# A Mamba state laid out in halves: another partition order and another cut of the replicated loads

## The chip, the cores and the metric

The kernel runs on one core of a Trainium2 chip. The metric is the device time of one execution, in microseconds; lower is better. Its engines are named as in the profile: PE (matrix multiply), DVE (vector), ACT (scalar and activation), POOL (GpSimd), and SP, which here only issues DMAs.

## The reference, cut to what matters

Four layers follow each other on an input of 2 x 128 x 128 x 128 float32: a convolution with a small Mamba scan and a group norm, a gate from window statistics, the first layer's form again with other weights, and a residual block of two 3x3 convolutions. The change is in the Mamba scan, which runs in the first and the third layer. At each of the 2 x 128 x 128 positions the 128 channels are taken as 8 tokens of 16 features; a token has 32 inner features d and each of these 16 states n:

```python
seq = y.reshape(B * H * W, 8, 16)
...
dA = jnp.exp(dt[..., None] * A)                       # (N, 8, 32, 16)
dBx = dt[..., None] * Bm[:, :, None, :] * xc[..., None]
def step(h, inp):
    a, b, c = inp
    h = a * h + b
    return (h, jnp.sum(h * c[:, None, :], axis=-1))
_, ys = jax.lax.scan(step, h0, (dA, dBx, Cm))         # over the 8 tokens
ym = ys + D * xc
```

So B and C of a token depend on n alone, u = dt * xc on d alone, and the state on both.

## The kernel before, in words

A tile is 4 rows of the picture, 512 positions; there are 64 tiles in a scan and 128 in the two. The 32 x 16 = 512 states of a token stand as 4 planes (j) of 128 partitions. A partition holds one state n and one e of 8 (d is split into j and e); `_state(e)` says which 16 partitions belong to e. Constants and weights that are prepared ahead take their columns from it: `neg`, `red` and `alog`.

The state needs u spread over n and B, C spread over e. The kernel does it with DMAs through HBM: `store` (L382, L389) writes u into the scratch tensor `su` (8 DMAs of 64 KB) and B and C into `sb` (2 DMAs); `load` reads them back for each of the tokens 0 to 6, replicated, into `ur` (128 partitions x 4 x 512) and `bcr` (128 x 2 x 512). Before, 112 partitions hold 16 states times 7 values of e, and the last 16 hold the eighth e, so that each of the two tiles is loaded by a DMA of 112 and one of 16 partitions (L435, L436 for `ur`; L439, L440 for `bcr`).

For a token t the steps are:
- `inject` (L445, POOL): h = ur * B, one instruction over 128 x 2048;
- `decay` (L454 on PE, L463 on ACT): exp(dt * A) into PSUM, two tiles `set`;
- `token` (L472, L473, L477, DVE): for each half of the planes, the decayed state, its product with C into `r`, and the sum with the injected part into `h`. L477 of token t reads what `inject` of token t wrote; L472 of the first token reads what `inject` of token 0 wrote;
- `gather` (L492, PE): the sum over n.

The order of work on every engine is written out by hand: each step has a due time in units of a token (LOAD_AT, INJECT_AT and so on, 7 a tile), and the instructions are issued in that order. Loads are due 3.7 tokens before the tile's clock, injects 1.8 before; the store of a tile is due just ahead of its first load. All these DMAs are issued by SP, in order. `ur` has 3 buffers, `bcr` 5, `h` 4. A DMA waits for its buffer and its source, and also for the eighth DMA before it, since eight completion lanes are used in turn. After the conv, the projections and softplus (PE, ACT) of the next tile fill the gaps.

Of the kernel before, what the change touches and what calls it, by code (L numbers as in the profile page):

```python
# [31 lines left out]
P = 128  # L32
NT, FT = 8, 16
DI, DS, DC = 32, 16, 4
NQ = 4
NJ = DI * DS // P
DJ = DI // NJ
NG = 4
CG = P // NG
WIN = 8  # L40
ROWS = 4
NS = ROWS * P
# [7 lines left out]
def _constants(H):  # L50

    parts = {}

    neg = np.zeros((NJ, NQ, DJ, NQ, P), np.float32)
    red = np.zeros((P, NQ, NQ, DJ), np.float32)
    gsum = np.zeros((2, NQ, DS, 2, NJ, NQ, DJ), np.float32)
    for q in range(NQ):
        for e in range(DJ):
            neg[:, q, e, q, _state(e)] = -1.0
            red[_state(e), q, q, e] = 1.0  # L60
        for g in range(2):
            gsum[g, q, :, g, :, q, :] = 1.0
    parts["neg"] = neg.reshape(P, -1)
    parts["red"] = red.reshape(P, -1)
    parts["gsum"] = gsum.reshape(P, -1)
    parts["group"] = np.kron(np.eye(NG), np.full((CG, CG), 1.0 / CG)).astype(np.float32)
    parts["ident"] = np.eye(P, dtype=np.float32)
    parts["neghalf"] = np.full((P, CG), -0.5, np.float32)
    return _packed(parts)


def _state(e):


    return np.arange(DS) + P - DS if e == DJ - 1 else np.arange(DS) * (DJ - 1) + e


def _bilinear(n):
# [38 lines left out]
def _mamba_layout(w):  # L117
# [5 lines left out]
    def half(a):  # L123

        a = a.reshape(*a.shape[:-2], 2, NQ, NJ, DJ)
        return np.ascontiguousarray(np.swapaxes(a, -3, -2)).reshape(*a.shape[:-4], 2 * P)
# [18 lines left out]
    for q in range(NQ):  # L145
        pdt1[:, q, :, :, q, :] = by_d[0][:, :, None, None]
        pdt2[:, q, :, :, q, :] = w["dt_proj_w"][:, 0].reshape(NJ, DJ)[None, None, :, :]
        pb[:, q, :, q, :] = by_d[1 : 1 + DS].transpose(1, 2, 0)
        pc[:, q, :, q, :] = by_d[1 + DS :].transpose(1, 2, 0)
        for e in range(DJ):  # L150
            alog[:, q, e, q, _state(e)] = w["A_log"].reshape(NJ, DJ, DS)[:, e, :]
# [137 lines left out]
def _mamba(tc, src, w, con, dst, scratch, stats, H):  # L289


    nc = tc.nc
# [136 lines left out]
    def load(k, t):  # L429

        s = live[k]
        n = P - DS
        ur = s["ur", t] = st.tile([P, NJ, NS], F32, tag="ur", name="ur", bufs=3)
        u = s["su"][t]
        nc.sync.dma_start(out=ur[:n], in_=u[: DJ - 1].unsqueeze(0).to_broadcast([DS, DJ - 1, NJ, NS]))  # L435
        nc.sync.dma_start(out=ur[n:], in_=u[DJ - 1].unsqueeze(0).to_broadcast([DS, NJ, NS]))  # L436
        m = s["bc", t] = st.tile([P, 2, NS], F32, tag="bcr", name="bcr", bufs=5)
        b = s["sb"][t]
        nc.sync.dma_start(out=m[:n], in_=b.unsqueeze(1).to_broadcast([DS, DJ - 1, 2, NS]))  # L439
        nc.sync.dma_start(out=m[n:], in_=b)  # L440

    def inject(k, t):
        s = live[k]
# [103 lines left out]
    x1, z1 = ahead(1)[0], behind(1)[0]  # L547
    order = [(0, band)] + taps(0, 0, 9) + [(0, turn)] + x0 + taps(1, 0, 3) + dt0 + taps(1, 3, 5) + bc0
    order += [(0, load, 0), (0, load, 1), (0, load, 2)]
    order += z0 + taps(1, 5, 9) + [(1, turn), (0, decay, 1), (0, inject, 0), (0, inject, 1)] + own0  # L550
    order += x1[:2] + z1[:2]
# [7 lines left out]
    for k in range(len(src) * ntile):  # L559
# [20 lines left out]
        for t in range(NT - 1):  # L580
            put(k, LOAD_AT + t, load, t)
            put(k, INJECT_AT + t, inject, t)
# [37 lines left out]
def _gates(tc, src, w, con, y, stats, wm, b1, up, dst, H):  # L620
# [6 lines left out]
    with tc.tile_pool(name="dg", bufs=2) as dp, tc.tile_pool(name="dg1", bufs=1) as sp, tc.tile_pool(  # L627
# [58 lines left out]
        def gram(b, y0):  # L686
# [3 lines left out]
            pg = s["pg"] = psg.tile([P, 2, 512], F32, tag="pg", name="pg")  # L690
            tiles = [(a, a * P // 2, g * CG) for g in range(NG) for a in range(2)]
            for a, pa, c0 in tiles:
# [414 lines left out]
```

## Time and profile before

| What | Value |
|---|---|
| Median of 3 runs | 7580.34 us (7578.54 to 7589.2) |
| Span of the profiled execution | 7571.5 us |
| DVE busy | 7011.8 us, 93% |
| PE busy | 6319.0 us, 83% |
| POOL busy | 5499.8 us, 73% |
| ACT busy | 4282.3 us, 57% |
| DMA queue of SP | 568672 packets, 1747.28 MB, 88.1% of 16 engines |
| `ur` loads, issue to landing | 11.5 us (112 partitions, 896 KB), 11.1 us (16, 128 KB) |
| `bcr` loads, issue to landing | 11.7 us (112 partitions, 448 KB), 11.0 us (16, 64 KB) |

The span runs from the first to the last instruction of one profiled execution; the page gives that execution's time by its span alone, and the median of the runs is 8.8 us above it. Busy shares are averages over the whole span, the two scans and the stages between and after them. A group's row has its line, engine, operation, tiles and count, then busy time and mean ns of one, and last the time that the engine was idle just before such instructions, with what ended most of it. The share of a DMA queue is the time that its packets took, of sixteen engines' span.

### The profile page before, as it was taken

Reading aid. Unit: us, or ns where it says so; the run is one execution under the profiler, and the core shown is the slowest. Engines: PE = TensorE matmul, PEld = TensorE weight load, DVE = VectorE, ACT = ScalarE, POOL = GpSimd, SP = SyncE. Lnnn points to the kernel's source line nnn. Section 1 sums busy time; section 2 is a strip of 40 time slices with the busy share of each in tenths; the row PEclk is TensorE's granted clock in tenths of the full one; section 3 lists DMA queues with packets and bytes.
Section 4 is the critical chain, followed back from the end, with each engine's and each line's share of the span. In section 5 each row is a group of like instructions: output and inputs, shape, how many; then the busy total and the mean of one; then the engine's idle time right before and its main releaser. Section 6 shows DMA issues by size and latency. Waiting matters only on the chain.

```text
span 7571.5 us, 89536 instructions
## 1 busy us (share of the span) xinstructions
PE 6319.0 (83%) x30416; PEld 2335.1 (31%) x30416; DVE 7011.8 (93%) x7114; ACT 4282.3 (57%) x4877; POOL 5499.8 (73%) x1783
## 2 busy tenths in 40 slices
PE   7888888888888888867788888888888888887994
PEld 2222222222222222224222222222222222223873
DVE  5999999999999999978699999999999999999986
ACT  5666666666656656545556666666656655662222
POOL 5878777877787778754578777877787778775541
PEclk8999999999999999978899999999999999997997
DMA  8999999999999999954799999999999999996604
GB/s 204 252 251 252 251 250 246 256 251 253 246 248 254 250 243 249 245 194 173 193 249 247 250 250 249 250 256 246 249 252 252 251 245 253 249 253 199 207 7 172
DMA packets 573738, 1769.80 MB, mean 234 GB/s; under 512 B 85568, under 2 KB 239712, under 8 KB 458208
## 3 DMA queue, kind: packets, MB, share of 16 engines
q1 hardware_dynamic: 568672, 1747.28, 88.1%
q10 hardware_dynamic: 4608, 16.78, 0.6%
q8 instruction: 242, 3.96, 0.2%
q14 instruction: 216, 1.77, 0.1%
HBM read 1552.83 MB, written 210.89 MB: 233 GB/s over the span
## 4 chain that ended last, share of the span: by engine, by line
DVE 41%; DMA 25%; PE 19%; issue 7%; ACT 5%; POOL 2%; SPq 1%; POOLq 0%; DVEq 0%; ACTq 0%
DMA bcr<-sb 19%; DVE set L472 14%; DVE h L477 12%; DVE r L473 12%; PE m L911 6%; DMA ur<-su 3%; PE one L350 2%; PE set L454 2%; ACT set L463 2%; PE ys L492 2%; PE one L400 2%; POOL h L445 2%; DVE v L505 1%; PE ys L483 1%; ACT xc L357 1%
## 5 line engine op out<-in xcount | busy, mean ns | idle before, releaser
L445 POOL TENSOR_TENSOR h<-ur,bcr 128x2048 f32<-128x2048 f32 x896 | 4060.7, 4539 | 1257.0 <-DMA bcr<-sb 1096.1
L472 DVE TENSOR_TENSOR set<-set,h 128x1024 f32<-128x1024 f32 x1792 | 2193.5, 1224 | 267.6 <-ACT set L463 165.4
L473 DVE TENSOR_TENSOR r<-set,bcr 128x1024 f32<-128x1024 f32 x1792 | 2194.5, 1225 | 61.5
L463 ACT ACTIVATE set<-set 128x1024 f32<-128x1024 f32 x1792 | 1745.9, 1006 | 870.0 <-PE set L454 856.6
L477 DVE TENSOR_TENSOR h<-set,h 128x1024 f32<-128x1024 f32 x1536 | 1866.0, 1215 | 28.1 <-POOL h L445 27.8
L454 PE MATMUL set<-dt,rep 32*128 32x512 f32 x7168 | 1402.9, 675 | 104.9 <-DVE h L477 98.1
L492 PE MATMUL ys<-r,ct 128*32 128x512 f32 x7168 | 1172.5, 635 | 36.4 <-DVE r L473 36.1
L323 PE MATMUL one<-band,conv 128*128 128x512 f32 x2304 | 1081.3, 605 | 21.9 <-DMA band<-in_x_dram 12.6
L454 PEld LDWEIGHTS set<-dt,rep 32*128 32x128 f32 x7168 | 405.1, 193 | 1002.3 <-issue 468.1
L400 PE MATMUL one<-xc,keep 128*64 128x512 f32 x1008 | 322.4, 723 | 462.1 <-ACT xc L357 355.5
L323 PEld LDWEIGHTS one<-band,conv 128*128 128x128 f32 x2304 | 406.6, 189 | 668.0 <-issue 596.8
L911 PE MATMUL m<-comb,u 128*128 128x256 f32 x2304 | 507.8, 381 | 46.0 <-DVE comb L904 44.8
L483 PE MATMUL ys<-t,ct 128*128 128x512 f32 x512 | 322.6, 716 | 252.3 <-DVE v L505 250.7
L911 PEld LDWEIGHTS m<-comb,u 128*128 128x128 f32 x2304 | 436.2, 190 | 117.3 <-issue 54.5
L492 PEld LDWEIGHTS ys<-r,ct 128*32 128x32 f32 x7168 | 181.2, 112 | 929.2 <-issue 759.6
L352 ACT ACTIVATE xc<-one,keep 128x512 f32<-128x512 f32 x252 | 173.4, 688 | 509.2 <-PE one L350 504.2
L374 POOL TENSOR_TENSOR u<-dt,xc 128x1024 f32<-128x1024 f32 x128 | 302.8, 2365 | 98.0 <-ACT dt L368 98.0
L420 PE MATMUL one<-prod,ct 128*128 128x512 f32 x504 | 280.8, 640 | 109.1 <-POOL prod L412 78.8
L350 PE MATMUL one<-y,w_in 128*128 128x512 f32 x504 | 341.1, 765 | 1.6 <-ACT xc L352 1.6
L463 ACT ACT_TABLE_LOAD x254 | 325.9, 1283 | 4.5
L427 POOL TENSOR_TENSOR t<-t,xc 128x1024 f32<-128x1024 f32 x128 | 302.4, 2363 | 10.0
L364 PE MATMUL one<-xc,w_dt 128*128 128x512 f32 x504 | 306.4, 692 | 2.7 <-ACT bc L407 2.7
(167 smaller groups left out, 5901.7 us busy)
## 6 DMA issues: line engine op xcount, KB each, us to landing
ur<-su SPq DMA_DIRECT2D x896, 896.0 KB, 11.5
bcr<-sb SPq DMA_DIRECT2D x896, 448.0 KB, 11.7
ur<-su SPq DMA_DIRECT2D x896, 128.0 KB, 11.1
su<-u SPq DMA_DIRECT2D x1024, 64.0 KB, 3.4
sb<-bc SPq DMA_DIRECT2D x256, 224.0 KB, 2.7
bcr<-sb SPq DMA_DIRECT2D x896, 64.0 KB, 11.0
y<-o SPq DMA_DIRECT2D x128, 256.0 KB, 9.3
band<-in_x_dram SPq DMA_DIRECT2D x28, 640.0 KB, 10.9
```

The costliest lines, as they stand in the source:

```text
L323: nc.tensor.matmul(py.rearrange("p (r w) -> p r w", r=ROWS), lhsT=w["conv"][:, tap, :], rhs=xb[:, r + kh : r + kh + ROWS, kw : kw + P], st ...
L350: nc.tensor.matmul(p, lhsT=w[("in", "z")[i]][:, g, :], rhs=s["y"], start=True, stop=True)
L400: nc.tensor.matmul(p[g * NQ * DS : (g + 1) * NQ * DS, :], lhsT=w[("xb", "xcm")[i]], rhs=s["xc"][:, g, :], start=True, stop=True,)
L445: nc.gpsimd.tensor_tensor(b, s["ur", t], s["bc", t][:, 0].unsqueeze(1).to_broadcast([P, NJ, NS]), ALU.mult)
L454: nc.tensor.matmul(a[j // 2][:, j % 2, :], lhsT=w["rep"][r, q, :], rhs=s["dt"][r, g, :], start=True, stop=True, tile_position=(r.start, 0),)
L463: nc.scalar.activation(x, x, AF.Exp)
L472: nc.vector.tensor_tensor(pt, pt, s["h", t - 1][:, js, :], ALU.mult)
L473: nc.vector.tensor_tensor(s["r", t][:, js, :], pt, s["bc", t - 1][:, 1].unsqueeze(1).to_broadcast([P, 2, NS]), ALU.mult)
L477: nc.vector.tensor_tensor(s["h", t][:, js, :], pt, s["h", t][:, js, :], ALU.add)
L483: nc.tensor.matmul(s["ys", g], lhsT=con["ident"], rhs=s["t1"][:, g, :], start=True, stop=False)
L492: nc.tensor.matmul(s["ys", g][a : a + NQ * DJ, :], lhsT=red[:, q, :], rhs=r[:, j, :], start=False, stop=(q == NQ - 1), tile_position=(0, a),)
L911: nc.tensor.matmul(m[:, n // 2, n % 2], lhsT=u[:, i, kw, :], rhs=v[:, i, :, kw : kw + P], start=(kw == 0), stop=(kw == 2),)
```

## The change

`_state` puts the eight e into two halves of 64 partitions, each 16 states by 4 values of e (NE = 4). `load` then issues five DMAs a token in place of four, in another order: the lower half of `bcr` in two quarters of 32 partitions, the upper half of `ur`, its lower half, and the upper half of `bcr`. Line numbers from there on move by a few.

```diff
+NE = DJ // 2
...
 def _state(e):
-    return np.arange(DS) + P - DS if e == DJ - 1 else np.arange(DS) * (DJ - 1) + e
+    return P // 2 * (e // NE) + NE * np.arange(DS) + e % NE
...
     def load(k, t):
         s = live[k]
-        n = P - DS
+        half, part = P // 2, P // 4
         ur = s["ur", t] = st.tile([P, NJ, NS], F32, tag="ur", name="ur", bufs=3)
-        u = s["su"][t]
-        nc.sync.dma_start(out=ur[:n], in_=u[: DJ - 1].unsqueeze(0).to_broadcast([DS, DJ - 1, NJ, NS]))
-        nc.sync.dma_start(out=ur[n:], in_=u[DJ - 1].unsqueeze(0).to_broadcast([DS, NJ, NS]))
         m = s["bc", t] = st.tile([P, 2, NS], F32, tag="bcr", name="bcr", bufs=5)
-        b = s["sb"][t]
-        nc.sync.dma_start(out=m[:n], in_=b.unsqueeze(1).to_broadcast([DS, DJ - 1, 2, NS]))
-        nc.sync.dma_start(out=m[n:], in_=b)
+        u, b = s["su"][t], s["sb"][t]
+        for at in (0, part):
+            rows = b[at // NE : (at + part) // NE]
+            nc.sync.dma_start(
+                out=m[at : at + part], in_=rows.unsqueeze(1).to_broadcast([part // NE, NE, 2, NS])
+            )
+        for at, e in ((half, NE), (0, 0)):
+            nc.sync.dma_start(
+                out=ur[at : at + half], in_=u[e : e + NE].unsqueeze(0).to_broadcast([DS, NE, NJ, NS])
+            )
+        nc.sync.dma_start(out=m[half:], in_=b.unsqueeze(1).to_broadcast([DS, NE, 2, NS]))
```

The change is described with the words "in halves of 64 and quarters of 32 partitions, four per DMA engine".

## The prediction

> **What bounds the kernel now.** I read the page first: shares by engine, the DMA queue, and the groups of the lines that touch the two replicated tiles.
>
> ```profile
> PE 6319.0 (83%) x30416; PEld 2335.1 (31%) x30416; DVE 7011.8 (93%) x7114; ACT 4282.3 (57%) x4877; POOL 5499.8 (73%) x1783
> ...
> q1 hardware_dynamic: 568672, 1747.28, 88.1%
> ...
> L445 POOL TENSOR_TENSOR h<-ur,bcr 128x2048 f32<-128x2048 f32 x896 | 4060.7, 4539 | 1257.0 <-DMA bcr<-sb 1096.1
> L472 DVE TENSOR_TENSOR set<-set,h 128x1024 f32<-128x1024 f32 x1792 | 2193.5, 1224 | 267.6 <-ACT set L463 165.4
> L473 DVE TENSOR_TENSOR r<-set,bcr 128x1024 f32<-128x1024 f32 x1792 | 2194.5, 1225 | 61.5
> ...
> L477 DVE TENSOR_TENSOR h<-set,h 128x1024 f32<-128x1024 f32 x1536 | 1866.0, 1215 | 28.1 <-POOL h L445 27.8
> ```
>
> Two things look full, DVE and DMA. The stretches that hold only the two scans tell them apart (columns: stretch, length, PE, PEld, DVE, ACT, POOL busy, clock, DMA share, GB/s):
>
> ```profile
> 162.00:3316.00 3154.00, 2686.97 (x11002) 845.50 (x10998) 3035.18 (x2680) 1890.02 (x2146) 2468.65 (x712) 0.94 0.96 248
> 3762.00:6890.00 3128.00, 2667.87 (x10964) 837.64 (x10962) 3016.22 (x2667) 1888.99 (x2143) 2468.26 (x710) 0.95 0.97 249
> ```
>
> The first stretch is 63 tiles, 50.1 us each. DVE is idle for 118.8 us in it (3154.0 less 3035.2) and 111.8 in the second. The waits in the first stretch say what for, and what POOL waits for:
>
> ```profile
> DVE set L472 <- ACT set L463: 73.3, 90, 1.5
> DVE h L477 <- POOL h L445: 6.4, 6, 2.3
> ...
> POOL h L445 <- DMA bcr<-sb: 476.3, 185, 6.7
> ```
>
> So the loads make POOL wait, but POOL makes DVE wait for almost nothing. DVE sets the time; the loads are late against POOL and just in time for DVE. What can be gained is what L477 lost to POOL, 27.8 us in the whole span (the page's row), 0.37%. The 165.4 us behind ACT follow from the order on PE and ACT, which the change leaves alone. What can be lost has no such bound.
>
> **How near the loads are to setting the time.** Both scans repeat, so one tile serves. These are the SP queue, and below it POOL, at one boundary between tiles (start, us, what):
>
> ```profile
> 5462.94 7.84 SPq L382 DMA_DIRECT2D su<-u  x8
> 5470.88 0.86 SPq L389 DMA_DIRECT2D sb<-bc  x2
> 5471.85 0.55 SPq L435 DMA_DIRECT2D ur<-su  x1
> 5472.45 0.58 SPq L436 DMA_DIRECT2D ur<-su  x1
> 5474.38 0.55 SPq L439 DMA_DIRECT2D bcr<-sb  x1
> 5474.98 0.58 SPq L440 DMA_DIRECT2D bcr<-sb  x1
> ```
>
> ```profile
> 5482.16 4.55 POOL L445 TENSOR_TENSOR h<-ur,bcr 128x2048 f32<-128x2048 f32 x1 [4.29 <-DMA bcr<-sb]
> 5488.11 4.54 POOL L445 TENSOR_TENSOR h<-ur,bcr 128x2048 f32<-128x2048 f32 x1 [1.40 <-DMA bcr<-sb]
> ```
>
> When the stores of u have landed, ur's loads go out; bcr's go out only when the store of B and C has landed too (L439 waited for sb 153.4 us in all, 171 times). The first and second injects of the tile then wait 4.29 and 1.40 us for bcr. I took, from the timeline, for 122 tiles the time from the end of these two injects to the DVE instruction that reads them: for the first, median 7.1 and lowest 1.6; for the second, median 3.3, a tenth of the tiles under 0.2. This slack is the whole margin.
>
> The rate of the engines, in the same boundary:
>
> ```profile
> 5473.50:5474.50 1.00, 1.00 (x4) 0.27 (x2) 0.97 (x2) 0.00 (x0) 1.00 (x1) 1.00 0.81 336
> 5480.00:5484.00 4.00, 1.17 (x11) 0.34 (x12) 3.97 (x5) 3.74 (x5) 1.84 (x1) 1.00 1.01 253
> ```
>
> With one 112-partition load in flight a busy engine moves 336/(16 x 0.81) = 25.9 GB/s; with several loads mixed, 253/(16 x 1.01) = 15.7. The scan as a whole has 248/(16 x 0.96) = 16.1. [...]
>
> **The change, part by part.** *The partition order* moves columns of constants and weights prepared ahead. Shapes and counts on PE, ACT, DVE and POOL stay: nothing.
>
> *Five DMAs a token in place of four*: 896 more issues at about 0.57 us (547 ns for the first of a tile, 580 for the next), 4.0 us of SP a tile. SP issues some 20 us of a 50.1 us tile, and waits the rest, so in the middle of a tile this is hidden. Each DMA also waits for the eighth before it; eight were two tokens and become 1.6. The loads of tokens 4 to 6 are issued as soon as POOL frees a buffer, and POOL is then back to back, so I charge nothing there.
>
> *bcr ahead of ur.* At the tile's start this counts. SP is in order: all five loads now stand behind the wait for sb, where ur used to go out ahead of it. After that wait two issues followed, now five: 3 x 0.57 = 1.7 us later for the last load of token 0. Behind it stand token 1's loads.
>
> *Bytes per engine.* Before, every load gave all 16 engines the same rows: (896 + 128 + 448 + 64)/16 = 96 KB a token (KB per issue from the page's list of DMA issues). By the change's own words a load gives each engine four partitions, so a 32-partition load uses eight engines. With rows of 8 KB in ur and 4 KB in bcr, and both quarters on the same eight, these have 8 x 8 + 12 x 4 = 112 KB, the other eight 8 x 8 + 4 x 4 = 80 KB. The 16 KB more cost 0.6 us a token at 25.9 GB/s and 1.0 at 16.1.
>
> *Contention* is the term that the trace does not show. The other DMAs of a tile are 8 x 64 + 2 x 224 + 256 + 640/2 = 1536 KB, 96 KB an engine, 6.1 us at 16.1. The heavier eight engines then need, a tile:
> - at 25.9 throughout: 7 x 4.4 + 6.1 = 37 us, hidden;
> - at today's 16.1: 7 x 7.1 + 6.1 = 56 us, 6 over the tile;
> [...]
>
> Even is (50.1 - 6.1)/7 = 6.3 us for 112 KB, 18.3 GB/s. [...] I take half of the 80 KB as contested: 72 KB at 25.9 and 40 KB at 13 is 6.0 us, 48 us a tile. It stays hidden, by 4%.
>
> [...]
>
> *The sum.* Token 0 and 1 land 1.7 + 0.6 = 2.3 us later. Setting that against each tile's slack (the lower of the two injects), DVE loses 53 us in 122 tiles (39 of them short), 55 in 126. The first tile of each scan has no slack (DVE waits for POOL there, 97.2 us in two waits) and takes the 2.3 twice: 60 in all. The same sum gives 16 us at a delay of 1.0, and 152 at 4.0. The profiled execution's span of 7571.5 would be 7631.5; the median of the runs is 8.8 above the span, so 7580.3 + 60 = 7640 us. Faster packets take something back, later stores (which wait for loads in flight) add; I leave both in the range.
>
> **The rivals.**
>
> *Contention falls and wins.* The tail load on 16 partitions goes, each engine writes four partitions in a row, and with rates well over 18.3 the older loads clear before the stores, whose issue now waits 7.84 us in the tile shown. Token 0 would land earlier and L477's 27.8 us go: 7553 to 7565. For it: a rate of 25.9 is possible. Against: the 1.7 us of issue are certain.
>
> *Nothing that counts.* The 2.3 us are paid back by faster packets down to under 1 us: within 15 us.
>
> *The heavier eight engines become the bound*, decided at 18.3 GB/s. [...]
>
> **How the numbers follow.** About 0.2% (15 us) is what a measurement here can tell from no change. Delay at the tile's start, +16 to +160: 0.47. Faster by 15 to 28: 0.20. No change: 0.20. Bound by eight engines, above +160: 0.13. So faster 0.20, same 0.20, slower 0.60. The range runs from 7556, most of the gain, to 7740, the delay of 4 us; it leaves out the last case and the edge of the gain. The likeliest case alone is 7596 to 7740, its value 7640.
>
> **What the new profile would show.** Right: the first inject's wait for DMA grows by 1 to 4 us a tile, L477's wait for POOL from 27.8 to 50–100, DVE's busy time the same, DMA share lower than 0.96 since eight engines idle. Wrong: L477's wait near nothing (the gain); POOL waiting for DMA in tokens 2 to 6 as well and tiles of 52 us or more (the eight engines).

## The result, and the profile after

The changed kernel takes 7913.92 us (median of 4 runs) against 7584.77 for the kernel before in the same runs: a ratio of 1.0426, 95% interval 1.0397 to 1.0455, some 329 us slower. The direction was forecast, the size was not: 7640 had been expected, and the range ended at 7740. The profiled execution's span is 7902.4 us.

From the page after, the groups that were shown of before (columns as there), and from the list of waits the way by which a late POOL reaches PE:

```profile
L451 POOL TENSOR_TENSOR h<-ur,bcr 128x2048 f32<-128x2048 f32 x896 | 4058.6, 4536 | 1714.1 <-DMA bcr<-sb 1203.1
L478 DVE TENSOR_TENSOR set<-set,h 128x1024 f32<-128x1024 f32 x1792 | 2194.3, 1224 | 363.0 <-ACT set L469 254.5
...
L483 DVE TENSOR_TENSOR h<-set,h 128x1024 f32<-128x1024 f32 x1536 | 1867.1, 1216 | 245.7 <-POOL h L451 244.9
```

```profile
PE one L421 <- POOL prod L413: 405.5, 108, 7.3
```

The same wait before:

```profile
PE one L420 <- POOL prod L412: 78.8, 42, 4.8
```

The mean times of POOL's, ACT's and DVE's instructions stayed (4539 and 4536 ns for the inject, 1006 and 1006 for ACT's decay, 1224 and 1224, 1215 and 1216 for DVE's rows shown). DVE now waits 244.9 us for POOL at L483 (27.8 at L477 before) and 254.5 for ACT at L478 (165.4 before): 217 and 89 more, 306 of the 331 us that the span grew. The second belongs, at least for a good part, to the first: PE's matmuls on `prod`, which POOL makes, waited 405.5 us where before they waited 78.8, and behind them stand, in order, the decays that ACT and then DVE need. PE's own matmuls became longer too (L454, now L460, from 675 to 714 ns on average, at a mean granted clock of 0.929 before and 0.895 after); how much of ACT's delay comes from that was not separated.

The same two stretches of the scans:

```profile
167.00:3472.00 3305.00, 2722.32 (x11000) 867.53 (x10996) 3040.65 (x2679) 1888.99 (x2146) 2468.26 (x712) 0.91 0.86 236
3921.00:7236.00 3315.00, 2738.05 (x11004) 867.59 (x11004) 3039.93 (x2683) 1889.18 (x2147) 2467.36 (x710) 0.90 0.86 235
```

A tile takes 52.5 us instead of 50.1 in the first. The DMA share fell from 0.96 to 0.86, but that is a mean over sixteen engines. By the prediction's count eight of them carry 7 x 112 + 96 = 880 KB a tile where the mean is 768; if that holds and packets take alike on all engines, their own share is about 0.86 x 880/768 = 0.99 (an estimate). So the mean alone does not clear the eight. The SP queue and POOL at one boundary between tiles show where time is lost:

```profile
5712.10 8.29 SPq L383 DMA_DIRECT2D su<-u  x8
5720.48 0.86 SPq L390 DMA_DIRECT2D sb<-bc  x2
5723.89 1.46 SPq L439 DMA_DIRECT2D bcr<-sb  x2
5725.45 1.19 SPq L443 DMA_DIRECT2D ur<-su  x2
5726.69 0.59 SPq L446 DMA_DIRECT2D bcr<-sb  x1
```

```profile
5734.59 4.54 POOL L451 TENSOR_TENSOR h<-ur,bcr 128x2048 f32<-128x2048 f32 x1 [6.57 <-DMA bcr<-sb]
5741.26 4.50 POOL L451 TENSOR_TENSOR h<-ur,bcr 128x2048 f32<-128x2048 f32 x1 [2.12 <-DMA bcr<-sb]
```

The last store is issued by 5721.3, and nothing follows until 5723.9, 2.6 us, because bcr's quarters wait for sb. Before, ur went out 0.1 us after the stores. The first inject then waits 6.57 us instead of 4.29. What the sixteen engines do in the 2.6 us behind the stores and in the 2.1 us that follow (columns as in the stretches above), before and after:

```profile
5471.80:5474.40 2.60, 1.54 (x4) 0.68 (x4) 2.57 (x4) 0.00 (x0) 2.60 (x2) 1.00 0.91 316
5474.40:5476.50 2.10, 2.10 (x12) 0.46 (x10) 2.10 (x3) 0.69 (x1) 2.10 (x1) 1.00 0.92 263
```

```profile
5721.30:5723.90 2.60, 2.60 (x11) 0.49 (x9) 1.14 (x2) 0.60 (x1) 2.60 (x2) 0.70 0.57 176
5723.90:5726.00 2.10, 2.10 (x14) 0.61 (x10) 2.07 (x3) 0.68 (x2) 2.10 (x1) 1.00 0.15 60
```

Share times length is 4.3 us before and 1.8 after: the engines run almost empty once the stores are through, and 2.5 us of their time are lost at this boundary. Over the whole span SP's first load of bcr (L439 in both kernels; before, ur went ahead of it) waited for sb, before and after:

```profile
SPq L439 <- DMA sb<-bc: 153.4, 171, 2.4
```

```profile
SPq L439 <- DMA sb<-bc: 311.6, 143, 2.5
```

On the engines that the new loads were said to use, one line bears:

```profile
DMA packets 573756, 1769.94 MB, mean 224 GB/s; under 512 B 85568, under 2 KB 239712, under 8 KB 458208
```

Before, the list of issues has 5330 DMAs, and 16 x 5330 = 85280 is nearly the whole number of packets under 512 B, 85568. That number is the same after, although 896 DMAs were added: 896 x 16 are made up for by 1792 quarters with eight fewer. So a quarter has eight such packets where other DMAs have sixteen. Read as one for each engine, which no trace shows directly, that is eight engines for a quarter, as the prediction took it; which eight, the trace does not tell.

### The profile page after: what moved, and what is told of

Read it like the earlier page. It is cut to its first block, busy times and chain, and to the rows that moved or that the text cites. A ratio compares the mean times of both kernels' runs of the same rounds, so it can differ in the third digit from the quotient of the medians.

```text
span 7902.4 us, 91850 instructions
## 1 busy us (share of the span) xinstructions
PE 6416.3 (81%) x30416; PEld 2383.6 (30%) x30416; DVE 7030.8 (89%) x7114; ACT 4278.9 (54%) x4877; POOL 5498.4 (70%) x1783
## 2 busy tenths in 40 slices
DMA packets 573756, 1769.94 MB, mean 224 GB/s; under 512 B 85568, under 2 KB 239712, under 8 KB 458208
## 3 DMA queue, kind: packets, MB, share of 16 engines
q1 hardware_dynamic: 568672, 1747.28, 79.8%
## 4 chain that ended last, share of the span: by engine, by line
DMA 54%; PE 16%; DVE 14%; SPq 5%; POOL 4%; issue 4%; ACT 3%; DVEq 0%; POOLq 0%; ACTq 0%
DMA bcr<-sb 31%; DMA ur<-su 17%; PE m L917 6%; DVE set L478 4%; DVE h L483 4%; DVE r L479 3%; POOL h L451 3%; SPq L439 3%; DMA su<-u 2%; SPq L443 2%; PE set L460 2%; PE one L351 2%; ACT set L469 1%; DMA sb<-bc 1%; PE ys L498 1%
## 5 line engine op out<-in xcount | busy, mean ns | idle before, releaser
L451 POOL TENSOR_TENSOR h<-ur,bcr 128x2048 f32<-128x2048 f32 x896 | 4058.6, 4536 | 1714.1 <-DMA bcr<-sb 1203.1
L478 DVE TENSOR_TENSOR set<-set,h 128x1024 f32<-128x1024 f32 x1792 | 2194.3, 1224 | 363.0 <-ACT set L469 254.5
L479 DVE TENSOR_TENSOR r<-set,bcr 128x1024 f32<-128x1024 f32 x1792 | 2194.2, 1224 | 61.5
L469 ACT ACTIVATE set<-set 128x1024 f32<-128x1024 f32 x1792 | 1740.4, 1006 | 740.3 <-PE set L460 666.9
L483 DVE TENSOR_TENSOR h<-set,h 128x1024 f32<-128x1024 f32 x1536 | 1867.1, 1216 | 245.7 <-POOL h L451 244.9
L460 PE MATMUL set<-dt,rep 32*128 32x512 f32 x7168 | 1430.8, 714 | 101.9 <-DVE h L483 96.4
L498 PE MATMUL ys<-r,ct 128*32 128x512 f32 x7168 | 1115.0, 641 | 16.8 <-DVE r L479 16.3
L460 PEld LDWEIGHTS set<-dt,rep 32*128 32x128 f32 x7168 | 413.2, 202 | 1010.5 <-issue 586.4
L421 PE MATMUL one<-prod,ct 128*128 128x512 f32 x504 | 329.1, 740 | 415.2 <-POOL prod L413 405.5
L422 ACT COPY t<-one 128x512 f32<-128x512 f32 x252 | 147.9, 587 | 627.0 <-PE one L421 627.0
L365 PE MATMUL one<-xc,w_dt 128*128 128x512 f32 x504 | 328.0, 737 | 2.7 <-ACT bc L408 2.7
```

The source lines that it names most:

```text
L451: nc.gpsimd.tensor_tensor(b, s["ur", t], s["bc", t][:, 0].unsqueeze(1).to_broadcast([P, NJ, NS]), ALU.mult)
L460: nc.tensor.matmul(a[j // 2][:, j % 2, :], lhsT=w["rep"][r, q, :], rhs=s["dt"][r, g, :], start=True, stop=True, tile_position=(r.start, 0),)
L469: nc.scalar.activation(x, x, AF.Exp)
L478: nc.vector.tensor_tensor(pt, pt, s["h", t - 1][:, js, :], ALU.mult)
L479: nc.vector.tensor_tensor(s["r", t][:, js, :], pt, s["bc", t - 1][:, 1].unsqueeze(1).to_broadcast([P, 2, NS]), ALU.mult)
L483: nc.vector.tensor_tensor(s["h", t][:, js, :], pt, s["h", t][:, js, :], ALU.add)
```

## The experiments

Theory A, formed from this trace, is a lap: POOL makes u, SP stores it, the first loads land, POOL injects, and in its own order only then makes the u of the next tile. A delay anywhere in it comes again in every tile. The rivals: B, eight engines with 112 KB set the pace; C, collisions between loads of 64 partitions do; D, the delay is met once per tile by the slack that the tile shows, as the prediction summed it.

For every kernel I took the lap from its timeline (mean of 118 tiles, us): from the end of u to the first inject of its tile; POOL's own work from there to the end of the next u; and POOL's idle time in that part. Their sum is the lap. It is, by the way it is taken, the time of a tile, so it follows the kernel's time whatever the cause; what can speak for a theory is which part changed.

| Kernel | Time | u to inject | work | idle | lap |
|---|---|---|---|---|---|
| before | 7580 | 23.6 | 21.9 | 5.0 | 50.4 |
| changed | 7914 | 26.1 | 21.9 | 5.2 | 53.2 |
| E1 ur first | 7768 | 24.8 | 21.9 | 5.6 | 52.2 |
| E2 before, bcr first | 8100 | 26.7 | 21.8 | 6.2 | 54.7 |
| E3 lower half whole | 8147 | 26.8 | 21.8 | 6.5 | 55.1 |
| E4 sb first | 7621 | 23.8 | 21.9 | 5.2 | 50.9 |
| E5 sb early | 7572 | 23.5 | 21.9 | 5.2 | 50.6 |
| E6 before, sb early | 7526 | 18.3 | 21.9 | 10.0 | 50.2 |
| E7 lower half whole, sb first | 7835 | 24.4 | 21.9 | 6.5 | 52.8 |
| E8 upper quarters too | 8318 | 28.0 | 21.8 | 6.6 | 56.3 |
| E9 before, three idle DMAs | 7544 | 22.7 | 21.9 | 5.7 | 50.3 |
| E10 before, six | 7708 | 25.0 | 21.9 | 4.6 | 51.5 |
| E11 ur first, sb early | 7527 | 18.3 | 21.9 | 10.0 | 50.2 |
| E12 stores ahead | 7717 | 24.8 | 21.9 | 4.9 | 51.6 |

One step of A does not fit the changed kernel. There u ends 3.6 us (mean) before SP issues the first store, and SP's first store waits for earlier loads to land, hardly ever for u:

```profile
SPq L383 <- DMA ur<-su: 516.5, 495, 2.5
...
SPq L383 <- POOL u L375: 56.7, 2, 29.6
```

So if a lap sets the pace there, it does not run over POOL's u. It may close in SP's queue itself: stores, loads, and the wait of later loads and of the next stores for the eighth DMA before them (of the changed kernel's 6180 DMAs whose completion lane was that of the eighth before, none went out until that one had landed, and half went out within 0.1 us of it). None of the experiments was made for that lap.

**E1, ur ahead of bcr, the pieces as changed.** (Here and below `q1`, `q2` are the quarters of bcr, `uh`, `ul` the halves of ur, `bh` the upper half of bcr.)

```diff
-        q1, q2, uh, ul, bh
+        uh, ul, q1, q2, bh
```

> The changed kernel with ur's two halves issued ahead of bcr's three loads; the pieces stay the same. Theory A, the lap: POOL makes u, SP stores it, the first loads land, POOL injects, and only then makes the next u. This lap was about 1.2 us a tile shorter than DVE's tile (POOL waited 151 us in all for DVE) and the change made it some 4 us longer, 1.7 of it because all five loads stand behind the wait for sb. With ur ahead these 1.7 us come back: 126 x 1.7 = 214 us off, 7914 to about 7700. Theory B, the heavy eight: eight engines carry 112 KB a token and set the pace whatever the order: 7890 to 7940. Theory C, collisions of halves: the order of the pieces decides which engines meet; no lap is needed, and the time can go either way by over 100 us, with the first token's wait unchanged near 6.9 us.

Measured: 7768.03 us, 1.0251 (1.023 to 1.0272). 146 us come back, and the first inject's mean wait falls from 6.9 to 5.6 us. A gave the direction and some 70 us too much; B is out as the whole cause.

**E2, the order alone, on the kernel before.**

```diff
-        ur[:n], ur[n:], m[:n], m[n:]
+        m[:n], m[n:], ur[:n], ur[n:]
```

> The kernel before, its 112 and 16 partition loads kept, with bcr's two loads issued ahead of ur's. Theory A: four issues instead of two stand behind the wait for sb, 1.15 us, which is about the 1.2 us that the lap had to spare: 7585 to 7660, the first inject's wait for DMA up from 5.2 us by about one. Theories B and C: the pieces and their engines are those of before, so 7585 within 15 us.

Measured: 8099.98 us, 1.0684 (1.0665 to 1.0702). The order alone costs 524 us, far more than even A had said. Waits of POOL and of SP's queue:

```profile
POOL h L445 <- DMA ur<-su: 1600.8, 458, 16.9
```

```profile
SPq L435 <- DMA sb<-bc: 313.1, 143, 3.8
```

The first load now goes out 3.6 us after the stores of u are issued, before 1.1: that is 2.5 us in which no load goes out, not the 1.15 us of issue that I had counted. The stores take 2.2 us more as well, since they wait for the landing of loads that are late themselves. The mean 8 KB packet took 523 ns, 497 before; whether collisions make a part of it is not shown. B and C, which gave no change at all, are out as the whole cause. With the same order the new pieces are the faster ones: 7914 against 8100.

**E3, the lower half of bcr in one load**, so that every engine has 96 KB.

```diff
-        q1, q2, uh, ul, bh
+        bl, uh, ul, bh          # bl: 64 partitions
```

> The changed kernel with the lower half of bcr in one load of 64 partitions instead of two of 32, so that all sixteen engines carry 96 KB a token in four loads of 64. Theory A alone: one issue fewer behind the wait for sb, 0.57 us a tile, about 7840. Theory B: the heavy eight are gone, 16 KB less on them, 0.6 to 1.0 us a token, so DVE binds again and the time comes to 7600 to 7700. [...]

Measured: 8146.65 us, 1.075 (1.0731 to 1.0768): 233 us slower than the quarters. B's forecast fails: the mean 8 KB packet takes 567 ns here, 470 in the changed kernel, 497 before, 14.4 GB/s an engine against 17.4 and 16.5. That would fit a part for C, but a collision itself is not shown. (B alone is not tested cleanly, since the edit slows the packets as it takes bytes away.)

**E4, the stores of B and C ahead of those of u**, everything else as changed.

```diff
     def store(k):
+        # the two DMAs to sb, then
         # the eight DMAs to su
-        # the two DMAs to sb
```

> The changed kernel with the two stores of B and C issued ahead of the eight of u; the loads keep their order. Theory A: bcr's first two loads no longer wait for a store that was issued last, and are under way while u's stores land; three issues instead of five stand behind the last store, 1.1 us, and the data of the quarters is already moved: 1.1 to 2 us a tile, 7914 to 7660-7780. Theory B and theory C: bytes, engines and order of the loads unchanged, 7890 to 7940.

Measured: 7621.01 us, 1.0056 (1.0042 to 1.007). The wait for sb is the loss: 293 of the 329 us go, with the bytes, engines and order of the loads unchanged. From its page:

```profile
L455 POOL TENSOR_TENSOR h<-ur,bcr 128x2048 f32<-128x2048 f32 x896 | 4061.2, 4539 | 1377.7 <-DMA bcr<-sb 985.1
...
L487 DVE TENSOR_TENSOR h<-set,h 128x1024 f32<-128x1024 f32 x1536 | 1866.6, 1215 | 76.7 <-POOL h L455 76.3
```

DVE's wait for POOL falls to 76.3 us from 244.9, and that for ACT fell with it, to 158.6 from 254.5, though nothing of ACT's was touched.

**E5, the changed kernel with sb stored two tokens earlier.**

```diff
+        put(k, -6.0, store_b)      # the two DMAs to sb
         put(k, STORE_AT, store)    # the eight DMAs to su
```

> The changed kernel, its five loads and their order kept, with the two stores of B and C taken out of the store step and issued some two tokens earlier, ahead of the loads of tokens 5 and 6 of the tile before. If the wait for sb at the head of the loads is the whole loss, the time comes back to that of the kernel before or a little below: two issues (0.8 us) leave the lap between u and the first inject as well, so that L477's waits for POOL fall to 30-80 us and the time is 7560 to 7610. If the bytes on eight engines or collisions carry a part, it stays above 7650.

Measured: 7571.93 us, 0.9999 (0.9985 to 1.0013). Without the wait for sb the new pieces are as fast as the kernel before with its own wait; the like comparison is E6.

**E6, the kernel before with the same early store.**

> The kernel before with the same early store of B and C, its 112 and 16 partition loads and their order kept. If the lap has the room that POOL's 151 us of waiting for DVE suggests, DVE binds already and only L477's 27.8 us can go: 7550 to 7585. If the lap sets the time in the kernel before too, over 30 us go.

Measured: 7526.12 us, 0.9942 (0.993 to 0.9954): faster than both kernels, and by more than the 27.8 us that the prediction had as the most that could be gained. What is left of POOL's waits for these loads:

```profile
POOL h L448 <- DMA bcr<-sb: 108.8, 64, 11.5
```

1096.1 us before. From u to the first inject it is 18.3 us now, which is POOL's own back-to-back work; POOL waits for ACT instead, and a tile takes 50.2 us:

```profile
POOL prod L415 <- ACT bc L410: 836.9, 115, 9.6
```

So the kernel before was not bound by DVE alone: the loads' start cost it 49 us, 0.4 us a tile.

**E7, E3's four loads with E4's store order.**

> The kernel with the lower half of bcr in one load of 64 partitions (four loads of 64 a token, 96 KB on every engine), with the stores of B and C issued ahead of those of u. If the eight engines with 112 KB were what costs, this is faster than the quarters with the same store order (7621): 7570 to 7600. If the quarters are there to keep sixteen engines from writing the same 64 partitions together, it is slower: the whole half cost 233 us more than the quarters with the store order unchanged, so 7700 to 7860.

Measured: 7834.78 us, 1.0343 (1.0318 to 1.0367), 214 us over E4. With the wait out of the way the quarters are worth nearly as much as before. The time lies in the range that was given for quarters that keep sixteen engines apart, but that this is the reason is not shown; shown are the packets, 567 ns for 8 KB here too, 470 in E4.

**E8, the upper half of bcr in quarters too.**

```diff
-        q1, q2, uh, ul, bh
+        q1, q2, uh, ul, q3, q4
```

> The changed kernel with the upper half of bcr in two loads of 32 partitions too, six loads a token. If all quarters run on the same eight engines these carry 128 KB a token and the others 64: 16 KB more at the 17.4 GB/s of the changed kernel (8 KB in 470 ns) is 0.9 us a token, of which the tokens that POOL waits for (0 to 4) put 1 to 4 us in the lap: 8040 to 8400. If a quarter of the upper half runs on the other eight, all carry 96 KB and the time is 7850 to 7950.

Measured: 8317.95 us, 1.0994 (1.0976 to 1.1013), 404 us over the changed kernel, in the range that was given for the same eight engines and far from that for the other eight. So all quarters, of the lower and the upper half, most likely use the same eight, which the trace does not show directly; the queue's share falls from 79.8% while the time grows:

```profile
q1 hardware_dynamic: 568672, 1747.28, 74.1%
```

**E9 and E10, three and six idle DMAs ahead of a tile's first load, on the kernel before.**

```diff
+        if t == 0:
+            for i in range(3):      # E10: 6
+                nc.sync.dma_start(out=idle[i], in_=s["bc"][:DS, 0, :P])
```

> The kernel before with three 8 KB DMAs that nobody reads, issued between a tile's stores and its first load: ur's first load goes out 3 x 0.36 = 1.1 us later, bcr's, which waits for sb until later than that, does not. Nothing else is changed. Theory A, the lap: what exceeds the lap's room recurs in every tile, so with no room left 1.1 x 126 = 139 us, with 1.2 us of room nothing: 7575 to 7715. Theory D, slack used once: the delay is set against the slack that each tile shows in the trace of the kernel before, 18 us for 1.1 us: 7590 to 7600.

> The same with six such DMAs: ur's first load goes out 2.2 to 2.5 us later (its completion lane then is that of the first store of sb), bcr's about one. Theory A: 2.2 to 2.5 us a tile less the room of 0 to 1.2: 126 to 315 us, 7700 to 7890, with the wait of DVE for POOL and for ACT up as in the changed kernel. Theory D: the slack of the tiles gives 50 to 60 us, 7625 to 7640.

Measured: E9 7544.32 us, 0.9938 (0.9917 to 0.996); E10 7708.48, 1.0164 (1.0136 to 1.0191). E10 lies in A's range and far from D's: the delay by six recurs, though a first load 2.9 us later made the tile only 1.1 us longer. E9 went the other way from both theories. Its first load does go out 1.5 us later, and its lap is shorter all the same:

```profile
POOL h L449 <- DMA bcr<-sb: 857.3, 340, 14.1
```

(1096.1 before.) ur and bcr now follow each other without the gap for sb, and the mean 8 KB packet takes 470 ns instead of 497. E10 has the same packets, 471 ns, and still loses. Why the packets are shorter with this start of the loads is not shown; which start is good was not tried out.

**E11, ur first and sb early, in the new pieces.**

> The changed kernel's pieces with ur's halves first and the stores of B and C issued some two tokens earlier. Theory A: the lap loses the wait for sb, and ur no longer stands behind bcr; with the quarters first this came to 7572, where POOL still waited 5.1 us for the first load. With ur first 7540 to 7580, the first inject's wait at most 5. If the order of the pieces matters by the collisions alone, it can be slower than 7572 by the stagger that the quarters in front give: 7600 to 7700.

Measured: 7527.05 us, 0.9919 (0.9897 to 0.9941). With ur ahead the new pieces reach the time of E6, 45 us below E5. The stagger by the quarters in front, which I had thought it might need, is not needed there.

**E12, one due time moved in the changed kernel.**

```diff
-STORE_AT = -4.15
+STORE_AT = -4.75
```

> The changed kernel with one due time moved: STORE_AT from -4.15 to -4.75, so that a tile's ten stores are issued ahead of the last load (token 6) of the tile before. The loads, their pieces, their order and their wait for sb stay. Theory A: the stores no longer stand behind five issues and behind the landing of those loads (u's end to the first store and the eight stores take 11.8 us in the changed kernel), the lap loses 2 us or more, and the loss of 2.8 us a tile goes for the most part: 7570 to 7720. Theory B or C, a pace set by bytes or collisions in the middle of the tile: 7880 to 7940.

Measured: 7717.44 us, 1.0186 (1.0161 to 1.021). The pieces stay and 196 us go, so B and C are out as the whole cause here too. But the wait for sb does not stay as expected: the loads of token 6 now fill the time between the stores and the first load, and SP waits 5.2 us for sb in all instead of 311.6. So this run takes away the same wait in another way, and does not test the lap at a point of its own. New is that the stores do wait for u here, in every tile:

```profile
SPq L383 <- POOL u L375: 342.2, 128, 30.0
SPq L439 <- DMA sb<-bc: 5.2, 3, 2.4
```

From u's end to the last store issued it is 5.5 us instead of 11.8, of which the loads, now later in the queue, give part back. DVE's wait for POOL halves:

```profile
DVE h L483 <- POOL h L451: 123.4, 126, 4.3
```

## Why the prediction was right or wrong, point by point

**What bounds the kernel: wrong.** "DVE sets the time" was read from waits in which POOL hardly held up DVE. Hardly any wait of DVE is no proof of room on POOL's side: the two can be of nearly one length. The kernel before stood at that corner: E6 and E11 gain 0.6 to 0.8% where "27.8 us" was given as the most, E2 loses 6.8%.

**The delay at the tile's start: the size right, partly by luck.** 2.3 us had been summed; u's end to the first inject grew by 2.5, and from the first store to it by 2.3 (20.1 to 22.5). Its terms were others: 1.7 us for three issues and 0.6 for bytes. The wait for sb itself is what ur now stands behind (first load 3.6 us after the stores of u instead of 1.1), and that is all of the 2.5: from the first load to the inject it is 10.7 us, 10.9 before. E4 and E5, which take the wait away, and E2, which brings it into the kernel before, show that term.

**What the delay costs: the step that failed.** The 2.3 us were set against each tile's slack as if every tile began with the slack of the old trace: 53 us in 122 tiles. The runs show a delay that comes again in every tile: u's end to the first inject is 2.5 us longer, the tile 2.8 us (50.4 to 53.2), and 2.8 x 126 is 348 us; measured were 329. A tile that starts late makes the next one late, so slack is used up once and not refilled. With the wait taken away 293 us (E4) and 342 us (E5) come back, and E10, with a delay put into the old kernel, loses 123 us where the slack gave 50 to 60. What hands the delay on from tile to tile stays open. POOL's u does not in the changed kernel, since its stores wait for loads and not for u; the waits of SP point at the queue itself, but no run cuts that path alone.

**Contention: not settled by the packets.** Half of 80 KB contested, at 13 GB/s, was 6.0 us for 112 KB, 429 ns for 8 KB. No run shows that term, neither the half nor the 13; what the runs show is the mean 8 KB packet, at 466 (E6) to 567 ns (E3), 17.6 to 14.4 GB/s. In the changed kernel it takes 470, 5% below the 497 before. That fall is not shown to come from the cut: with the old pieces E6 and E9 have 466 and 470, with the new ones E1 has 483. The rate of 25.9 GB/s was read as that of one load, but in that microsecond the 16-partition load was under way too and the stores of sb were landing. The pieces as such are little or no loss: E11 equals E6, E5 is 46 us above E6, and with the order of the change (E2) they save 186 us. With nothing but loads of 64 partitions (E3) the loss is 570 us, with 229 GB/s moved in a stretch of its first scan.

**The heavier eight engines.** As a pace of their own they are refuted by E4, E5 and E11: the same 880 KB a tile, by the prediction's count, go through in 50.9, 50.6 and 50.2 us. The sign that the prediction had set for them was met all the same: tiles of over 52 us, and POOL's mean wait before the injects of tokens 2 and 4 up from 0.3 and 0.1 us to 1.2 and 1.0. So that sign did not tell them from a late start. It is not excluded that they have too little to spare to make up for a late start: 880 KB in 50.2 us is 18.0 GB/s, about the 17.4 of the mean 8 KB packet. With 128 KB on eight engines, by the same count (E8), the time grows by 404 us.

**The rivals.** "Falls and wins" named the lever, a store that is cleared earlier, but tied it to packet rates; it was to be had by issuing sb earlier. That the five DMAs a token are hidden in the middle of a tile fits E11, which has five and the time of E6 with four.

## What to carry to other kernels

Before a delay is set against slack, follow the work of one period back to itself: if engines that work in order and an in-order queue of DMAs close a lap, a delay in it can come again in each period (here an inject 2.5 us later and tiles 2.8 us longer), and the slack shown is only what two laps of like length leave between them. Check each step of such a lap in the waits: here the step from u to its store was not one. Put the load whose source is ready first at the head of an in-order queue, and issue a small store as soon as its data exists: moving two 224 KB stores by two tokens took 342 us off the changed kernel and 49 off the kernel before. And look at the waits of the queue after each experiment: E12 was meant to leave the wait for sb in place, and did not.

## What the runs showed of the hardware that was not expected

- A load of 32 partitions has eight packets under 512 B where the others have sixteen (85568 in both kernels, with 896 DMAs more in the changed one). That this means eight engines, and the same eight whichever quarter is written, is inferred, the second from E8's 404 us.
- With loads of 64 partitions only, an engine got 14.4 GB/s over 8 KB (567 ns, E3 and E7), not the 13 that the prediction took for contested bytes; the new mixture got 17.4 (470 ns), the old one 16.5 (497 ns), and 17.6 (466 ns) with sb stored early (E6). So the start of the loads counts too, and not only how they are cut.
- Three DMAs of 8 KB that nobody reads made the kernel before 0.6% faster (E9). The wait for sb fell away and the packets became 5% shorter; why that start is the better one stays open.
